# Layer 0's softmax weights in PSUM, and both node products of a pair in one bank: a four-layer graph network on one core

## The chip, the core and the metric

The kernel runs on one core of a Trainium2 chip. A core has a matrix engine (PE, with its weight loads shown apart as PEld), a vector engine (DVE), a scalar engine (ACT), a GpSimd engine (POOL) and a queue that only starts transfers (SP). They run side by side, each in its own program order, and wait for one another through semaphores. SBUF is the working memory with 128 partitions; PSUM is a small second memory, used here in banks of 512 float32 values per partition, into which PE writes its results, and which DVE and ACT read and write.

The metric is the device time of one execution in microseconds (us), as the median of several runs. Beside it there is one execution taken by the hardware profiler, with the start and duration of every instruction.

## The reference, cut to what matters

Four residual graph layers work on 6250 nodes and 100000 edges that are sorted by their target node. Layer 0 is a graph attention layer with eight heads. The change touches this layer and the work that prepares layer 1 from its result:

```python
h = jnp.maximum(_layernorm(x, axis=-1), 0.0)
x = x + _L0_gnn_ref(h, src, dst, ...)
# inside _L0_gnn_ref, after its own norm and x = x @ W_in + b_in:
scores_u = x @ W_u + b_u
scores_v = x @ W_v
e = scores_u[src] + scores_v[dst]
e = jnp.where(e >= 0, e, NEG_SLOPE * e)
m = jax.ops.segment_max(e, dst, num_segments=N_NODES)
ex = jnp.exp(e - m[dst])
s = jax.ops.segment_sum(ex, dst, num_segments=N_NODES)
probs = ex / s[dst]
xh = x.reshape(N_NODES, HEAD_DIM, N_HEADS)
msg = xh[src] * probs[:, None, :]
agg = jax.ops.segment_sum(msg, dst, num_segments=N_NODES)
return agg.reshape(N_NODES, DIM) @ W_ff + b_ff
# and then, for layer 1:
h = jnp.maximum(_layernorm(x, axis=-1), 0.0)
xw = h @ W
```

Layer 1 is a normalised sum over neighbours with a batch norm, layer 2 two single-head attention layers, layer 3 a pairwise interaction with a small network on the edges' attributes.

## The kernel before, in words

Nodes are ranked by their number of incoming edges and cut into 49 blocks of 128, one node per partition. `CAPS[b]` says how many neighbours a block holds per node: 44 for block 0, 25 for block 1, then falling to 9. For every block and neighbour slot one indirect transfer, issued by POOL, fetches 128 rows (one per partition) from a table in DRAM: `fetch` at L1623. It reads the 128 row numbers from a column of an index tile in SBUF (`k.ell` in layer 0). Layers 0, 1, 2a and 2b make 820 such fetches each, layer 3 another 882 of pair rows.

Layer 0 (L1627 to L1702) runs through `in_turns`, which interleaves three kinds of generators by hand. The order in which the generators emit instructions is the order on every engine; no scheduler rearranges them.

- `block0(b)`, one per block. First it issues the block's fetches into `rows` (three buffers; block 0 has a large one of its own). At the next block's first turn DVE forms the scores `e` of the fetched rows (L1656, L1657), their maximum (L1659) and the difference (L1660). One turn later ACT takes the exponential in place, `e` to `e`, both in SBUF (L1662). Another turn later DVE multiplies the rows by the weights (L1665, `rows` and `e`, result in `rows`), sums over the neighbours (L1669), sums the weights (L1670), and divides (L1671, L1673).
- `nodes0(b, a)`, one for each pair of blocks, appended to `tails` when the pair's sums are done. It multiplies the sums by `W_ff`, adds the result to the node rows `xp`, normalises, multiplies by layer 1's `W`, and writes layer 1's table `t1` (the profile's `l_t`). Each product is `times_in_hops`: transposes on PE into PSUM (L1092), three turns of waiting (`late`), a copy to SBUF on ACT (L1096), one turn, the matmul on PE (L1100), three turns. DVE reads the products from PSUM at L1640 and L1644.
- Background work through `behind`: `source_ranks`, which computes `k.ranks` for the next layers (its DVE lines L1372, L1374, L1375, L1386 and L1390 and PE line L1380), and from block 3 on `edge_weights`, the network on the edges for layer 3 (PE L1252 to L1274, ACT L1304 to L1315).

A block has `turns_of(b)` turns, four for most blocks, six for block 1. Layer 1's fetches read `t1`, so the first of them waits for the last pair's table rows.

PSUM in layer 0: `Banks(ps, 2, "g0_th")` holds two banks, taken in turn by successive products. A product's transposes lie in columns 0 to 255 of its bank, its matmul result in columns 256 to 511 of the same bank (`space=256`).

Layers 2a and 2b have the same block structure with one head. There ACT already writes the exponentials to a PSUM tile, and DVE's multiply (L1837) reads rows from SBUF and weights from PSUM:

```python
ex = weighed[:, b % 4, 0:n]
nc.scalar.activation(ex, e, AF.Exp, bias=s[:, 0:1])
e = ex
yield
v = rows[:, :n, 0:D]
nc.vector.tensor_tensor(v, v, e[:, :, None].to_broadcast([128, n, D]), op=ALU.mult)
```

Of the kernel before, what the change touches and what calls it, by code (L numbers as in the profile page):

```python
# [15 lines left out]
F32 = mybir.dt.float32  # L16
# [4 lines left out]
AF = mybir.ActivationFunctionType  # L21
# [6 lines left out]
N, D, E = 6250, 128, 100000  # L28
# [8 lines left out]
NH, HD = 8, 16  # L37
# [482 lines left out]
def load_cols(k, pool, a, name):  # L520
    t = pool.tile([D, a.shape[1]], F32, name=name)
    k.nc.sync.dma_start(t, a)
    return t
# [515 lines left out]
def norm_in_hops(k, p, x, got, name="nm"):  # L1039

    nc = k.nc
    nb = x.shape[1]
    mv = p.tile([128, nb, 2], F32, name=name + "_mv", bufs=3)
    for b in range(nb):
        st = p.tile([128, 6], F32, name=name + "_st")
        nc.vector.bn_stats(st, x[:, b, :])
        nc.vector.bn_aggr(mv[:, b, :], st)
    yield
    r = p.tile([128, nb, 2], F32, name=name + "_r", bufs=3)
    nc.scalar.activation(r[:, :, 0], mv[:, :, 1], AF.Sqrt, bias=k.eps)  # L1050
    yield
    nc.vector.reciprocal(r[:, :, 0], r[:, :, 0])
    nc.vector.scalar_tensor_tensor(r[:, :, 1], mv[:, :, 0], -1.0, r[:, :, 0], op0=ALU.mult, op1=ALU.mult)
    yield
    out = p.tile([128, nb, D], F32, name=name + "_h", bufs=3)
    got.append(out)
    for b in range(nb):
        nc.scalar.activation(out[:, b, :], x[:, b, :], AF.Relu, bias=r[:, b, 1:2], scale=r[:, b, 0:1])
    yield
# [22 lines left out]
        return self.tile[:, self.at]  # L1082


def times_in_hops(k, p, banks, h, w, width, got, late=1, space=512):

    nc = k.nc
    nb = h.shape[1]
    both = banks.next()
    t = both[:, 0:nb * 128].rearrange("p (b d) -> p b d", d=128)  # L1090
    for b in range(nb):
        nc.tensor.transpose(t[:, b, :], h[:, b, :], k.ident)  # L1092
    for _ in range(late):
        yield
    hT = p.tile([128, nb, 128], F32, name="th_T", bufs=3)
    nc.scalar.copy(hT, t[:, :nb, :])  # L1096
    yield
    y = both[:, space:512] if space < 512 else banks.next()
    for b in range(nb):
        nc.tensor.matmul(y[:, b * width:(b + 1) * width], lhsT=hT[:, b, :], rhs=w, start=True, stop=True)  # L1100
    got.append(y[:, 0:nb * width].rearrange("p (b f) -> p b f", f=width))
    for _ in range(late):
        yield


def with_scores(k, c, ps, w, scores, name):

    nc = k.nc
    n = sum(a.shape[1] for a in scores)
    full = c.tile([D, D + n], F32, name=name)  # L1110
    nc.sync.dma_start(full[:, 0:D], w)
    a = c.tile([D, n], F32, name=name + "_a")
    at = 0
    for s in scores:
        nc.sync.dma_start(a[:, at:at + s.shape[1]], s)
        at += s.shape[1]
    ty = ps.tile([128, 512], F32, name="tm_ty")
    nc.tensor.transpose(ty[:, 0:128], full[:, 0:D], k.ident)
    wT = c.tile([D, D], F32, name=name + "_t")
    nc.vector.tensor_copy(wT, ty[:, 0:128])  # L1120
    y = ty[:, 128:128 + n]
    nc.tensor.matmul(y, lhsT=wT, rhs=a, start=True, stop=True)
    nc.vector.tensor_copy(full[:, D:D + n], y)
    return full, a
# [375 lines left out]
def step(line):  # L1500

    return next(line, DONE) is not DONE


def finish(line):
    while step(line):
        pass
# [48 lines left out]
def by_rank(k, table, rows, b, nb=1):  # L1556

    k.nc.sync.dma_start(table[b * 128:(b + nb) * 128, :].rearrange("(b l) f -> l b f", l=128), rows)


def fast_layers(k, x, src, edges, l0, l1, l2a, l2b, l3):


    nc, tc = k.nc, k.tc
    gamma, beta, w_in, b_in, w_u, b_u, w_v, w_ff, b_ff = l0
    with ExitStack() as ctx:
# [11 lines left out]
        wf = load_cols(k, c, w_ff, "wf")  # L1578
        bf = load_row(k, c, b_ff, "bf", 128)
        w1 = load_cols(k, c, l1[0], "w1")  # L1580
        b1, g1, e1 = (load_row(k, c, a, n, 128) for a, n in zip(l1[1:], ("b1", "g1", "e1")))
        b2, b3 = load_row(k, c, l2a[3], "b2", 128), load_row(k, c, l2b[3], "b3", 128)
        with tc.tile_pool(name="fw_ps", bufs=1, space=PSUM) as ps:
            w2, _ = with_scores(k, c, ps, l2a[0], [a.rearrange("(p o) -> p o", o=1) for a in l2a[1:3]], "w2")
            w3, _ = with_scores(k, c, ps, l2b[0], [a.rearrange("(p o) -> p o", o=1) for a in l2b[1:3]], "w3")
# [40 lines left out]

        with tc.tile_pool(name="g0s", bufs=1) as q, tc.tile_pool(name="g0s_ps", bufs=1, space=PSUM) as qs, \  # L1627
                tc.tile_pool(name="g0", bufs=2) as p, tc.tile_pool(name="g0_ps", bufs=1, space=PSUM) as ps:
            banks = Banks(ps, 2, "g0_th")
            bigs = big.enter_context(tc.tile_pool(name="g0b", bufs=1, side="right"))  # L1630

            tails, sums = [], {}

            def nodes0(b, a):
                nb = a.shape[1]
                y, h = [], []
                xb = xp[:, b:b + nb, 0:D]
                nc.vector.tensor_tensor(xb, xb, bf[:, None, :].to_broadcast([128, nb, D]), op=ALU.add)
                yield from times_in_hops(k, p, banks, a, wf, D, y, 3, 256)
                nc.vector.tensor_tensor(xb, xb, y[0], op=ALU.add)  # L1640
                yield from norm_in_hops(k, p, xb, h)
                yield from times_in_hops(k, p, banks, h[0], w1, D, y, 3, 256)
                o = own[:, b:b + nb, 0:D]
                nc.vector.tensor_tensor(o, y[1], dinv[:, b:b + nb, None].to_broadcast([128, nb, D]), op=ALU.mult)  # L1644
                by_rank(k, t1[0:NP, :], o, b, nb)

            def block0(b):
                n = CAPS[b]
                nc.gpsimd.indirect_dma_start(
                    out=xp[:, b, :], out_offset=None, in_=xv,  # L1650
                    in_offset=bass.IndirectOffsetOnAxis(ap=k.node_i[:, b:b + 1], axis=0))
                rows = rows_tile(p, b, WE, D + NH, "g0_x", bigs)
                fetch(rows, t0, k.ell, b)
                yield
                e = (bigs if b == 0 else p).tile([128, n if b == 0 else WE, NH], F32, name="g0_e" + "b" * (b == 0))[:, :n, :]
                nc.vector.tensor_tensor(e, rows[:, :n, D:D + NH], xp[:, b, None, D:D + NH].to_broadcast([128, n, NH]), op=ALU.add)  # L1656
                nc.vector.scalar_tensor_tensor(e, e, SLOPE, e, op0=ALU.mult, op1=ALU.max)  # L1657
                s = p.tile([128, 3, NH], F32, name="g0_s")
                nc.vector.tensor_reduce(s[:, 0, :], e.rearrange("p w h -> p h w"), axis=AX.X, op=ALU.max)  # L1659
                nc.vector.tensor_tensor(e, e, s[:, 0:1, :].to_broadcast([128, n, NH]), op=ALU.subtract)  # L1660
                yield
                nc.scalar.activation(e, e, AF.Exp)  # L1662
                yield
                v = rows[:, :n, 0:D].rearrange("p w (d h) -> p w d h", h=NH)
                nc.vector.tensor_tensor(v, v, e[:, :, None, :].to_broadcast([128, n, HD, NH]), op=ALU.mult)  # L1665
                if b % 2 == 0:
                    sums[b // 2] = p.tile([128, min(2, NR - b), D], F32, name="g0_a")
                a = sums[b // 2][:, b % 2, :]
                nc.vector.tensor_reduce(a, rows[:, :n, 0:D].rearrange("p w d -> p d w"), axis=AX.X, op=ALU.add)  # L1669
                nc.vector.tensor_reduce(s[:, 1, :], e.rearrange("p w h -> p h w"), axis=AX.X, op=ALU.add)  # L1670
                nc.vector.reciprocal(s[:, 2, :], s[:, 1, :])  # L1671
                ah = a.rearrange("p (d h) -> p d h", h=NH)
                nc.vector.tensor_tensor(ah, ah, s[:, 2:3, :].to_broadcast([128, HD, NH]), op=ALU.mult)  # L1673
                if b % 2 or b == NR - 1:
                    tails.append(nodes0(b // 2 * 2, sums[b // 2]))

            ranks = source_ranks(k, q, qs)
            step(ranks)
            names = Pace(ranks, 0.22)

            def behind(b):
                if b == 3 and not hasattr(back, "weights"):
                    big.close()
                    begin_weights()
                    back.pace = Pace(back.weights, 0.07, 3, NR - 1)
                names(b)
                if hasattr(back, "pace"):
                    back.pace(b)

            in_turns([block0(b) for b in range(NR)], turns_of, behind, tails)  # L1690
            finish(ranks)
        named.close()
# [3 lines left out]
        with tc.tile_pool(name="g1s", bufs=1) as q, tc.tile_pool(name="g1s_ps", bufs=1, space=PSUM) as qs, \  # L1696
                tc.tile_pool(name="g1", bufs=2) as p:
            both = qs.tile([128, 512], F32, name="g1_both")
# [59 lines left out]
            with tc.tile_pool(name="g1_ps", bufs=1, space=PSUM) as ps:  # L1758
                banks = Banks(ps, 3, "g1_th")
# [30 lines left out]
        for name, table, bias in (("g2", t2, b2), ("g3", t3, b3)):  # L1790
            with tc.tile_pool(name=name, bufs=2) as p, tc.tile_pool(name=name + "_big", bufs=1) as bigs, \
                    tc.tile_pool(name=name + "_ps", bufs=1, space=PSUM) as ps:
                banks = Banks(ps, 3, name + "_th")


                weighed = ps.tile([128, 4, 128], F32, name=name + "_w")
# [245 lines left out]
```

## Time and profile before

| what | value |
|---|---|
| median of 3 runs | 8062.21 us (8047.26 to 8094.31) |
| the profiled execution's own time | 6335.19 us |
| its span, first to last instruction | 6333.0 us |
| POOL busy in the span | 4280.4 us, 68% |
| DVE busy | 3821.8 us, 60% |
| PE busy | 2837.1 us, 45% |
| ACT busy | 1182.8 us, 19% |

The stages, read from the first and last start of each table's fetches:

| stage | from to (us) |
|---|---|
| ranking of nodes, first node products | 0 to 455 |
| layer 0, block 0's fetches | 455 to 514 |
| layer 0, the other fetches | 514 to 1632 |
| layer 0's last pairs, no fetch under way | 1632 to 1656 |
| layer 1 | 1656 to 2684 |
| layer 2a, 2b, 3 | 2780 to 6333 |

How to read the views: a group of instructions has its source line, engine, operation, the tiles `out<-in` and the count, then the total busy time in us and the mean of one in ns, then the idle time of the engine just before them and what ended it. "Issue" is idle time in which the engine waited for nothing that the profile shows. In a timeline a row begins with start and duration in us. In a table of stretches each engine has its busy time and number of instructions.

The profiled execution is 1727 us shorter than the median of the runs; the trace does not show where that difference lies.

### The profile page before, as it was taken

To read this page: it belongs to the slowest core of one execution; us is meant where nothing else is said; L and a number is where in the kernel's file an instruction comes from. 1 tells how busy PE (TensorE), PEld (TensorE's weight loads), DVE (VectorE), ACT (ScalarE), POOL (GpSimd) and SP (SyncE) were. 2 spreads that over 40 slices of the span, in tenths; PEclk is the share of its full clock that TensorE was granted. 3 is DMA by queue.
4 is the path that set the end of the run, shared out by engine and by line. 5 is a ranking of instruction groups with operands and counts; after the bars stand their busy time and mean duration, and the time that the engine had idled before them with its cause. 6 is when DMAs were issued, how large, how long until landed. Compare 5 with 4: busy or idle time off the path is not lost. (4 is left out here: it accounts for less than half of the span.)

```text
span 6333.0 us, 46143 instructions
## 1 busy us (share of the span) xinstructions
PE 2837.1 (45%) x14116; PEld 1979.1 (31%) x14116; DVE 3821.8 (60%) x7136; ACT 1182.8 (19%) x2136; POOL 4280.4 (68%) x4403
## 2 busy tenths in 40 slices
PE   2320244444464774046555453234444346556555
PEld 2210132333243552034434111011111135555555
DVE  9744555665346942244333896688888646666666
ACT  0110122333221221023333010122222201001010
POOL 0037777777677777737777776667766567777775
PEclk9655566666677877557766676566666577887877
DMA  0124333333332332233333223899999943333333
GB/s 6 52 54 77 84 94 91 98 94 85 68 91 80 95 101 76 50 54 88 90 90 83 56 57 46 173 201 196 199 186 185 181 102 100 100 100 99 99 99 75
DMA packets 444362, 626.13 MB, mean 99 GB/s; under 512 B 81071, under 2 KB 334802, under 8 KB 434259
## 3 DMA queue, kind: packets, MB, share of 16 engines
q0 software_dynamic: 159296, 397.56, 26.9%
q1 hardware_dynamic: 284433, 224.86, 16.3%
q8 instruction: 115, 1.88, 0.1%
q14 instruction: 154, 1.26, 0.1%
q10 hardware_dynamic: 364, 0.57, 0.0%
HBM read 441.86 MB, written 180.80 MB: 98 GB/s over the span
## 5 line engine op out<-in xcount | busy, mean ns | idle before, releaser
L1894 POOL DMA_INDIRECT fp_rows<-pair_rows,ids x882 | 873.0, 990 | 289.5 <-issue 254.7
L1623 POOL DMA_INDIRECT g_x<-l_t,ell x776 | 822.4, 1060 | 236.5 <-issue 233.8
L1623 POOL DMA_INDIRECT g_x<-l_t,ranks x820 | 777.7, 948 | 274.0 <-issue 245.5
L1623 POOL DMA_INDIRECT g_x<-l2b_t,ranks x776 | 738.3, 951 | 295.1 <-issue 212.7
L1488 PE MATMUL sr_acc<-sr_t,sr_l 128*128 128x441 f16 x1640 | 558.6, 498 | 844.8 <-DVE sr_l L1481 761.4
L1623 POOL DMA_INDIRECT g_x<-l2a_t,ranks x776 | 735.7, 948 | 236.4 <-issue 231.8
L1912 PE MATMUL fp_qe<-own,fp_ot 128*128 128x128 f32 x1764 | 338.1, 363 | 494.7 <-DVE fp_pr L1919 494.5
L1273 PEld LDWEIGHTS ew_ps<-ew_r,ew_g 128*125 128x125 f32 x1600 | 389.9, 284 | 537.3 <-issue 523.0
L1488 PEld LDWEIGHTS <-sr_l 128*128 128x128 f16 x1640 | 172.8, 120 | 1218.7 <-DVE sr_l L1481 1044.1
L1712 DVE TENSOR_REDUCE g_s<-g_x 128x128 f32<-128x2432 f32 (+16 forms) x50 | 185.0, 3700 | 468.9 <-DMA g_x<-l_t,ranks 468.9
L1912 PEld LDWEIGHTS fp_qe<-own,fp_ot 128*128 128x128 f32 x1764 | 301.4, 263 | 522.4 <-DVE fp_pr L1919 517.6
L1273 PE MATMUL ew_ps<-ew_r,ew_g 128*125 128x128 f32 x1600 | 441.5, 372 | 0.0
L1274 PE MATMUL ew_ps<-ew_s,ew_g 128*125 128x128 f32 x1600 | 437.1, 369 | 0.0
L1899 DVE TENSOR_TENSOR fp_oh<-iota_l,fp_rows 128x768 f32<-128x768 f32 x147 | 141.0, 959 | 458.9 <-DMA fp_rows<-pair_rows,ids 458.9
L1842 DVE TENSOR_REDUCE g_a<-g_x 128x128 f32<-128x2048 f32 (+13 forms) x96 | 389.2, 4054 | 3.3
L1480 DVE TENSOR_SCALAR sr_t<-sr_it,sp_tile 128x882 f16<-128x882 f16 x820 | 385.5, 470 | 0.0
L1274 PEld LDWEIGHTS ew_ps<-ew_s,ew_g 128*125 128x125 f32 x1600 | 370.3, 284 | 0.0
L1270 PE MATMUL ew_ps<-ew_bias,ew_three 65*125 65x512 bf16 x200 | 103.9, 519 | 524.8 <-ACT ew_out L1315 524.8
L1908 ACT COPY fp_ot<-fp_tr 128x768 f32<-128x768 f32 x147 | 117.4, 799 | 1117.2 <-PE fp_tr L1904 1113.7
L1481 DVE TENSOR_SCALAR sr_l<-sr_it,sp_lane,sr_w 128x128 f16<-128x128 f16 x820 | 302.9, 369 | 8.2 <-POOL sr_w L1456 8.2
L1304 ACT ACTIVATE ew_g<-ew_ps,ew_c 128x500 f32<-128x500 f32 x200 | 135.4, 677 | 832.6 <-PE ew_ps L1265 831.7
L1380 PE MATMUL rk_ps<-rank_b,rk_oh 128*128 128x49 bf16 x1640 | 76.1, 211 | 443.7 <-DVE rk_pr L1372 437.8
(318 smaller groups left out, 6400.9 us busy)
## 6 DMA issues: line engine op xcount, KB each, us to landing
edge_rows<-ew_out SPq DMA_DIRECT2D x50, 910.0 KB
rk_row<-src_lanes SPq DMA_DIRECT2D x82, 320.0 KB
fp_rows<-pair_rows,ids POOLq DMA_INDIRECT x882
g_x<-l_t,ranks POOLq DMA_INDIRECT x820
g_x<-l_t,ell POOLq DMA_INDIRECT x776
g_x<-l2a_t,ranks POOLq DMA_INDIRECT x776
g_x<-l2b_t,ranks POOLq DMA_INDIRECT x776
ew_a<-in_edge_attr_dram SPq DMA_DIRECT2D x25, 448.0 KB
```

The source lines that it names most:

```text
L1273: nc.tensor.matmul(y[:EP, u * D:(u + 1) * D], lhsT=g[:, 0, e], rhs=m.r2, start=False, stop=False)
L1274: nc.tensor.matmul(y[:EP, u * D:(u + 1) * D], lhsT=g[:, 1, e], rhs=m.s2, start=False, stop=(u == 3))
L1304: nc.scalar.activation(g[:, i, :], h[:, i, 0:4 * EP], AF.Silu, bias=b)
L1480: nc.vector.tensor_scalar(t[:, i, :], it, k.tile3[:, cc:cc + 1], None, op0=ALU.is_equal)
L1481: nc.vector.tensor_scalar(l[:, i, :], it[:, 0:128], k.lane3[:, cc:cc + 1], weight[:, cc % KG:cc % KG + 1], op0=ALU.is_equal, op1=ALU.mult)
L1488: nc.tensor.matmul(acc[:, h, 0:HT], lhsT=l[:, i, :], rhs=t[:, i, h * HT:(h + 1) * HT], start=(cc % KG == 0), stop=end)
L1623: nc.gpsimd.indirect_dma_start(out=rows[:, j, :], out_offset=None, in_=table, in_offset=bass.IndirectOffsetOnAxis(ap=ids[:, at:at + 1], ax ...
L1712: nc.vector.tensor_reduce(s, rows[:, :n, :].rearrange("p w d -> p d w"), axis=AX.X, op=ALU.add)
L1842: nc.vector.tensor_reduce(a, v.rearrange("p w d -> p d w"), axis=AX.X, op=ALU.add)
L1894: nc.gpsimd.indirect_dma_start(out=rows[:, t, :], out_offset=None, in_=k.pairs, in_offset=bass.IndirectOffsetOnAxis(ap=k.ids[:, at:at + 1] ...
L1899: nc.vector.tensor_tensor(oh, k.iota_l[:, None, :].to_broadcast([128, TG, 128]), rows[:, :, D + 1:D + 2].to_broadcast([128, TG, 128]), op= ...
L1912: nc.tensor.matmul(qe[:, t, :], lhsT=ot[:, t, :], rhs=k.own[:, h, 0:D], start=True, stop=True)
```

## The change

The exponentials of layer 0 go to a PSUM tile `weighed` of one bank. Even blocks use columns 0 to 255, odd blocks columns 256 to 511. The DVE multiply and the sum of the weights then read the weights from PSUM; the scores `e` stay in SBUF up to the exponential. Block 0's 44 neighbours with 8 heads take 352 columns.

The number of banks stays at two: `nodes0` no longer has two of its own but one, `room`. The first product uses columns 0 to 255, the second columns 256 to 511, and a matmul's result is written over the transposes that it was made from. `times_in_hops` loses its `space` argument and gets `room`; with `room=None`, as in layers 1 and 2, it takes two banks in turn as it did. The last block stands alone (49 is odd), and its `nodes0` now lets four turns pass before it begins.

```diff
-def times_in_hops(k, p, banks, h, w, width, got, late=1, space=512):
+def times_in_hops(k, p, banks, h, w, width, got, late=1, room=None):
+
 
     nc = k.nc
     nb = h.shape[1]
-    both = banks.next()
-    t = both[:, 0:nb * 128].rearrange("p (b d) -> p b d", d=128)
+    t = banks.next() if room is None else room
+    t = t[:, 0:nb * 128].rearrange("p (b d) -> p b d", d=128)
     for b in range(nb):
         nc.tensor.transpose(t[:, b, :], h[:, b, :], k.ident)
     for _ in range(late):
         yield
     hT = p.tile([128, nb, 128], F32, name="th_T", bufs=3)
-    nc.scalar.copy(hT, t[:, :nb, :])
+    nc.scalar.copy(hT, t)
     yield
-    y = both[:, space:512] if space < 512 else banks.next()
+    y = banks.next() if room is None else room
     for b in range(nb):
         nc.tensor.matmul(y[:, b * width:(b + 1) * width], lhsT=hT[:, b, :], rhs=w, start=True, stop=True)
...
-            banks = Banks(ps, 2, "g0_th")
+
+            weighed = ps.tile([128, 512], F32, name="g0_w")
+            room = ps.tile([128, 512], F32, name="g0_th")
...
             def nodes0(b, a):
                 nb = a.shape[1]
+                if nb < 2:
+
+                    for _ in range(4):
+                        yield
                 y, h = [], []
                 xb = xp[:, b:b + nb, 0:D]
                 nc.vector.tensor_tensor(xb, xb, bf[:, None, :].to_broadcast([128, nb, D]), op=ALU.add)
-                yield from times_in_hops(k, p, banks, a, wf, D, y, 3, 256)
+                yield from times_in_hops(k, p, None, a, wf, D, y, 3, room[:, 0:256])
                 nc.vector.tensor_tensor(xb, xb, y[0], op=ALU.add)
                 yield from norm_in_hops(k, p, xb, h)
-                yield from times_in_hops(k, p, banks, h[0], w1, D, y, 3, 256)
+                yield from times_in_hops(k, p, None, h[0], w1, D, y, 3, room[:, 256:512])
...
-                nc.scalar.activation(e, e, AF.Exp)
+                ex = weighed[:, b % 2 * 256:b % 2 * 256 + n * NH].rearrange("p (w h) -> p w h", h=NH)
+                nc.scalar.activation(ex, e, AF.Exp)
+                e = ex
                 yield
                 v = rows[:, :n, 0:D].rearrange("p w (d h) -> p w d h", h=NH)
                 nc.vector.tensor_tensor(v, v, e[:, :, None, :].to_broadcast([128, n, HD, NH]), op=ALU.mult)
```

## The prediction

> **What bounds the kernel now.** The page's chain of waits explains nothing here (its shares round to 0%), so I began with the groups of instructions and looked for the engine that never rests.
>
> ```profile
> L1623 POOL DMA_INDIRECT g_x<-l_t,ell x776 | 822.4, 1060 | 236.5 <-issue 233.8 <-DMA g_x<-l_t,ell 2.4 <-DMA g_x_big<-l_t,ell 0.3
> L1623 POOL DMA_INDIRECT g_x<-l_t,ranks x820 | 777.7, 948 | 274.0 <-issue 245.5 <-DMA l_t<-own 24.0 <-DMA g_x<-l_t,ranks 4.5
> L1623 POOL DMA_INDIRECT g_x<-l2b_t,ranks x776 | 738.3, 951 | 295.1 <-issue 212.7 <-DMA g_x<-l2b_t,ranks 54.3 <-DVE sr_l L1481 16.4
> L1623 POOL DMA_INDIRECT g_x<-l2a_t,ranks x776 | 735.7, 948 | 236.4 <-issue 231.8 <-DVE sr_l L1481 0.9 <-DVE g_s L1844 0.9
> ```
>
> One source line, four layers. All of POOL's idle time before layer 0's fetches is "issue", 0.30 us between any two, and its 776 fetches with those gaps fill 822.4 + 236.5 = 1059 us of the stage's 1118 (the other 59 are the 48 fetches of `xp`). So POOL sets the pace of layer 0. And layer 0's fetch costs 1060 ns on average where the other layers pay 948 to 951. The timeline shows why; first layer 0, then layer 2a:
>
> ```profile
> 803.23 2.82 DVE L1665 TENSOR_TENSOR g_x<-g_x,g_e 128x2560 f32<-128x2560 f32 x1
> 804.33 2.53 POOL L1623 DMA_INDIRECT g_x<-l_t,ell  x1 [0.30 <-issue]
> 807.17 0.94 POOL L1623 DMA_INDIRECT g_x<-l_t,ell  x1 [0.31 <-issue]
> ...
> 2899.19 3.49 DVE L1837 TENSOR_TENSOR g_x<-g_x,g_w 128x3200 f32<-128x3200 f32 x1 [0.35 <-ACT g_w L1833]
> 2899.26 0.94 POOL L1623 DMA_INDIRECT g_x<-l2a_t,ranks  x1 [0.30 <-issue]
> 2900.50 0.94 POOL L1623 DMA_INDIRECT g_x<-l2a_t,ranks  x1 [0.30 <-issue]
> 2901.75 0.94 POOL L1623 DMA_INDIRECT g_x<-l2a_t,ranks  x1 [0.30 <-issue]
> ```
>
> Under L1665, both of whose inputs lie in SBUF, a fetch that starts is held until 0.8 us after the multiply has ended. Under L1837, the same multiply with its weights in PSUM, three fetches start and none is held. I counted this over the whole trace: 51 fetches start inside the 49 L1665s and last together 74.9 us more than 51 times 944 ns (the undisturbed fetch); 173 start inside the 98 L1837s, and their excess is -0.1 us. Of the 90 us that layer 0's fetches last too long, another 14.0 go to the rank work (L1372 6.2, L1390 5.3, L1386 2.5), which the change leaves alone.
>
> Next I asked whether anything else could take over. DVE's waits in 514 to 1632:
>
> ```profile
> DVE g_e L1656 <- DMA g_x<-l_t,ell: 285.8, 33, 13.3
> DVE g_e L1656 <- DMA xp<-xv_t,node_i: 120.5, 12, 15.0
> DVE g_e L1656 <- issue: 11.1, 2, 5.9
> DVE g_x L1665 <- ACT g_e L1662: 13.8, 23, 1.7
> ```
>
> Columns: total, times, longest. DVE spends 431 us of the stage waiting, all but 13.8 for fetches: 9.0 us in each of 48 blocks. It is the follower. The same stretch by engine, and the stage's end:
>
> ```profile
> 514.00:1632.00 1118.00, 397.56 (x2797) 295.31 (x2796) 654.32 (x1035) 272.68 (x424) 867.00 (x824) 0.60 0.36 90
> ...
> 1653.23 0.29 DVE L1644 TENSOR_TENSOR own<-g_th,dinv 128x128 f32<-128x128 f32 x1 [1.18 <-PE g_th L1100]
> ...
> 1655.86 0.94 POOL L1623 DMA_INDIRECT g_x<-l_t,ranks  x1 [24.02 <-DMA l_t<-own]
> ```
>
> PE is busy 36%, ACT 24%, DVE 59%, the DMA engines 36%. Only at the end does POOL wait for the others, 24 us, until the last node product has come through and its rows are written.
>
> **What the Trainium skill says.** "SBUF — State Buffer", section "Who interferes with whom": a DVE instruction with two SBUF inputs takes its second one through the read port that it shares with GpSimd, and holds up a GpSimd instruction that reads SBUF until it has finished. The trace agrees in both directions (74.9 us under 49 multiplies, none under 98). "PSUM — Partial Sum Buffer", section "PSUM bank collisions raise a hardware error": two engines must be kept apart by bank, not by address. So sharing a bank means more semaphore waits, and I looked for these. "VectorE: DVE Perf Modes", sections on the perf-mode tiers and the errata: a float32 multiply of two tensors has one speed wherever its inputs lie; a PSUM source costs 120 cycles of fixed time instead of 58, 65 ns at 0.96 GHz. The trace shows not even those 65 ns on the multiply, at equal shape:
>
> ```profile
> L1837 DVE TENSOR_TENSOR g_x<-g_x,g_w 128x2048 f32<-128x2048 f32 x10 | 22.7, 2271 | 0.3 <-ACT g_w L1833 0.3
> L1665 DVE TENSOR_TENSOR g_x<-g_x,g_e 128x2048 f32<-128x2048 f32 x5 | 11.4, 2288 | 0.5 <-ACT g_e L1662 0.5
> ```
>
> **The change part by part.**
>
> 1. The weights leave SBUF (L1662, L1665). Removes 74.9 us from POOL, which has no slack in this stage: -74.9. What is late next: nothing for 9.0 us per block; after the change a block takes 1.5 us less, so DVE keeps 7.5 us. DMA traffic rises from 90 to some 97 GB/s, and layers 2b and later run at up to 188. Fetches will now stand otherwise against the rank work; that term is 14.0 us today, and a third of it either way, 4.7, goes into the range.
>
> 2. L1670 reads PSUM with a step of 8 values. No row shows that form. Below, nothing; above, 65 ns by the price named, 49 times: 3.2 us of DVE, covered by its 9.0 us per block. If the cover were gone, +3.2. L1665 is the same: 0 to 3.2. I take 0.
>
> 3. ACT writes PSUM. The exponentials are 263 to 370 ns; a destination nearer or farther changes tens of ns, 49 times, behind DVE waits: 0. In the built program the semaphore wait sits on the table load ahead of the exponential for 42 blocks instead of 34, so for 8 blocks a 1.28 us load no longer runs ahead of the scores: 10.3 us of later exponentials altogether, again inside 9.0 us per block: 0; cover gone, +10.3.
>
> 4. `weighed` is one bank for two blocks. A new exponential must not meet DVE's reading of the last. But it already waits for its own L1660, which stands behind the last block's L1670 in DVE's order. No new wait: 0.
>
> 5. One bank for the node products. Before, two banks in turn; pairs overlap, one's first product with the other's second. In the program's order on PE, ACT and DVE nothing moves except around the last block, and node instructions wait for essentially the same instructions: already before, L1640 waits for the other pair's L1100 that stands just ahead of it. A gain from a freed wait is excluded, since nothing is freed. I take 0. The upper end is the rival below: behind a waiting L1640 on DVE stand the next block's scores, and behind these its row buffer, which POOL needs three blocks later.
>
> 6. Four turns for block 48. This lies in the 24 us at the end, where every wait counts. Its first product now stands behind the second of pair 46, on all three engines. Working with the rows of that stretch: pair 46's add ends at 1644.9, its normalised transposes at 1648.6; then block 48's copy 0.27, matmul 0.8, pair 46's matmul 1.22 (1650.9); then block 48's add, norm, transpose, copy, matmul, about 4.0. Its L1644 starts near 1655 instead of 1653.23: +2 (0 to 5). SP's one table write moves with it.
>
> Sum: -74.9 + 2 = -72.9 us against the profiled execution, 6335.19 (a span of 6333.0 and 2.2 around it) to 6262.3. Later stages start earlier as a whole: their order is fixed, layer 1 is POOL's again (1027 of its 1028 us busy or issuing), so nothing waits there for an old date. The median is 8062.21, 1727 us more, and the trace does not say where. If these microseconds lie outside layer 0, the same 72.9 come off: 7989.3. If they stretch everything by 1.27, the gain lies between 66.6 - 2 (a fetch every 1.59 us meets the multiply 0.17 us later, 49 times) and 1.27 x 74.9 - 2 = 93.1. I take 7989; with the spread of the three runs, about 20 us, this case's own range is 7945 to 8020.
>
> **The rivals.**
>
> - Half the gain, 8026. In the longer executions behind the median POOL waits for landings or buffers in layer 0, and part of the stalls lies under these waits. For: 1727 unexplained us. Against: in the trace POOL waits for nothing in that stage.
> - No gain, 8064. The stall isn't from the second input in SBUF but from something else about layer 0's multiply (its 32-byte pattern, its rate of writing), so it stays, plus item 6. Against: L1837 writes the same shapes in the same time and stalls nothing.
> - Slower, 8127. One bank chains the products of two pairs: DVE waits for PE at L1640 and L1644, and PE is in the middle of the edge network. The longest wait of ACT for a node product today is 11.9 us (copy behind L1092); if DVE had to wait so long twice per pair, 23.8, it would use up its 18 per pair and the 3.1 that the change saves, and lose 2.7 in each of 24 pairs, 65 us. It decides from 21.1 us per pair. Against: DVE waits for PE at these two lines only some 1 us in that stage today, under nearly the same waits.
>
> **How the numbers follow.** Chances: full gain 0.72, half 0.12, none 0.08, slower 0.08. About 0.5%, 40 us, is what a measurement can tell from no change. Full gain gives faster (0.70, with 0.02 within 0.5%), half gain is split (0.06 and 0.06), none is within. Together: faster 0.76, same 0.16, slower 0.08. The range takes the first two cases, 7945 to 8045, and leaves the last two out.
>
> **What would show it right or wrong.** Right: layer 0's fetches at about 963 ns, which is (822.4 - 74.9) / 776 (the 14 us of rank work remain), none over 2 us under L1674, the multiply of the new file; layer 0's fetches end near 1557 and layer 1's first starts some 26 us later; everything after is shifted by about 73 us and otherwise alike. Step 5 is wrong if DVE's waits for PE at the node products grow beyond a few us, or POOL shows waits other than "issue" in layer 0. Step 6 is wrong if the gap before layer 1 is far from 26. The prediction fails if the fetches still last 2.5 us under the multiply, or if the span falls by 73 and the median doesn't.

## The result, and the profile after

| kernel | median of 6 runs | lowest to highest |
|---|---|---|
| before | 8078.49 us | 8047.26 to 8094.31 |
| after | 8172.28 us | 8144.0 to 8203.73 |

The ratio is 1.0119, with a 95% interval of 1.0084 to 1.0153: slower by 94 us, where 73 us less were forecast. Every job (a set of runs taken together on one chip) ran at one of two levels, with the kernel before at 6290 to 6370 us or at 8060 to 8180 us, and these timed runs are of the high level, while the profile that the prediction was read from, 6335.19 us, is of the low one.

The page of the changed kernel has two lines that answer to the first ones shown before, and the last one is the same fetch in layer 1:

```profile
span 8170.3 us, 46134 instructions
...
L1624 POOL DMA_INDIRECT g_x<-l_t,ell x776 | 746.2, 962 | 656.8 <-DVE g_s L1679 426.5
L1624 POOL DMA_INDIRECT g_x<-l_t,ranks x820 | 812.7, 991 | 458.9 <-issue 249.8
```

The fetch of layer 0 lasts 962 ns on average, as forecast (963): the hold under the multiply is gone. Yet POOL now idles 656.8 us before these fetches, 426.5 of them for DVE, which has not yet released a row buffer. In the profile that the prediction used, POOL waited for DVE nowhere in this stage. What DVE waits for in that stretch, 516 to 1978 us of the kernel after (total, times, longest):

```profile
DVE rk_pr L1373 <- remote: 435.1, 20, 45.6
DVE xp L1647 <- PE g_th L1101: 148.0, 15, 35.6
DVE rk_pr L1373 <- issue: 134.5, 5, 51.0
DVE xp L1647 <- remote: 66.2, 4, 20.5
```

The four rows and three smaller ones (one of them 26.7 us) are 812 us, and all are at lines that read a product of PE. "Remote" means that a semaphore was raised at that moment and that no instruction ends there. One such wait in the timeline of all engines:

```profile
1220.83 0.67 PE L1381 MATMUL rk_ps<-rank_b,rk_oh 128*128 128x49 bf16 x20
...
1223.92 0.66 DVE L1391 TENSOR_TENSOR rk_ob<-iota_l,rk_hi 128x490 f32<-128x490 f32 x1
...
1228.41 1.22 PE L1101 MATMUL g_th<-wf,th_T 128*128 128x128 f32 x4 [6.92 <-issue]
...
1252.57 0.94 POOL L1656 DMA_INDIRECT xp<-xv_t,node_i  x1 [0.30 <-issue]
1258.84 0.67 DVE L1373 TENSOR_TENSOR rk_pr<-rk_ps,rk_ob 128x490 f32<-128x490 f32 x1 [34.26 <-remote]
1258.90 0.37 ACT L1097 COPY th_T<-g_th 128x256 f32<-128x256 f32 x1 [26.95 <-remote]
...
1277.17 0.94 POOL L1624 DMA_INDIRECT g_x<-l_t,ell  x1 [23.65 <-DVE g_s L1679]
```

Read it from the bottom. POOL waits 23.65 us for a buffer. DVE could not release it, because it stood for 34.26 us at L1373, which multiplies a result of the rank matmuls. PE's last group of these began at 1220.83 and PE did only four node matmuls after it, so what L1373 needs was finished, by the records, over 35 us before L1373 ran. ACT, which waits for other results of PE, was let go 0.06 us after DVE. Both came 5.3 us after POOL's last fetch had ended. In layer 0 of this profile, 35 waits of DVE for PE are over 5 us; 20 of them end between 3.4 and 7.4 us after POOL's last fetch, when POOL has run out of buffers. Another 11 end during one of POOL's fetches or within 1.4 us of its end.

The ends of matmuls come from a model, but the trace also records when PE raised its semaphore. For the rank group above, whose end is put at 1221.5, the raise stands at 1258.82, 0.02 us before L1373 starts. In this stage, 61 of 221 of PE's raises aren't on record within 5 us of the modelled end; in e6 below, a run of the same kernel at the low level, it is 1 of 224. A tenth of PE's raises are missing from this trace (1130 of 1252 are there), too few to make up the 61.

So two questions stand: does the kernel before show the same waits when it runs at 8100 us, and which part of the change makes them cost more?

### The profile page after: what moved, and what is told of

It is laid out like the page before. It is cut to its first block, busy times and chain, and to the rows that moved or that the text cites. A ratio compares the mean times of both kernels' runs of the same rounds, so it can differ in the third digit from the quotient of the medians.

```text
span 8170.3 us, 46134 instructions
## 1 busy us (share of the span) xinstructions
PE 2969.3 (36%) x14116; PEld 2033.6 (25%) x14116; DVE 3796.8 (46%) x7136; ACT 1179.9 (14%) x2136; POOL 4239.5 (52%) x4403
## 5 line engine op out<-in xcount | busy, mean ns | idle before, releaser
L1624 POOL DMA_INDIRECT g_x<-l_t,ell x776 | 746.2, 962 | 656.8 <-DVE g_s L1679 426.5
L1624 POOL DMA_INDIRECT g_x<-l_t,ranks x820 | 812.7, 991 | 458.9 <-issue 249.8
L1274 PEld LDWEIGHTS ew_ps<-ew_r,ew_g 128*125 128x125 f32 x1600 | 409.0, 297 | 1823.5 <-issue 1808.0
L1928 DVE TENSOR_TENSOR fp_pr<-fp_rows,fp_qe 128x256 f32<-128x256 f32 x441 | 183.4, 416 | 702.1 <-remote 666.1
L1846 DVE TENSOR_TENSOR g_x<-g_x,g_w 128x2048 f32<-128x2048 f32 (+13 forms) x96 | 233.9, 2437 | 585.7 <-ACT g_w L1842 491.6
L1274 PE MATMUL ew_ps<-ew_r,ew_g 128*125 128x128 f32 x1600 | 461.9, 386 | 12.5 <-issue 12.5
L1275 PE MATMUL ew_ps<-ew_s,ew_g 128*125 128x128 f32 x1600 | 458.2, 383 | 21.4 <-issue 21.4
L1941 PE MATMUL fp_acc<-fp_ms,fp_oh 128*128 128x128 f32 x1764 | 327.2, 317 | 228.4 <-issue 223.9
L1275 PEld LDWEIGHTS ew_ps<-ew_s,ew_g 128*125 128x125 f32 x1600 | 390.4, 298 | 21.9 <-issue 21.9
L1941 PEld LDWEIGHTS fp_acc<-fp_ms,fp_oh 128*128 128x128 f32 x1764 | 282.6, 229 | 252.3 <-issue 247.4
```

What stands on the lines that cost most here:

```text
L1274: nc.tensor.matmul(y[:EP, u * D:(u + 1) * D], lhsT=g[:, 0, e], rhs=m.r2, start=False, stop=False)
L1275: nc.tensor.matmul(y[:EP, u * D:(u + 1) * D], lhsT=g[:, 1, e], rhs=m.s2, start=False, stop=(u == 3))
L1624: nc.gpsimd.indirect_dma_start(out=rows[:, j, :], out_offset=None, in_=table, in_offset=bass.IndirectOffsetOnAxis(ap=ids[:, at:at + 1], ax ...
L1928: nc.vector.tensor_tensor(pr, rows[:, two, 0:D], qe[:, two, :], op=ALU.mult)
L1941: nc.tensor.matmul(acc, lhsT=oh[:, t, :], rhs=ms[:, t, :], start=(t0 + t == 0), stop=(t0 + t == TB - 1))
```

## The experiments

The expectations take the level for a property of the chip. It isn't: e14 and e15 ran at the low level on the chips that had shown the high one in e11 and e1, and e16 the other way round on the chip of e4 and e5. "Theory A" has one bank as the culprit, B the later stages, C the stream of POOL's fetches that holds PE's results back, D the weights in PSUM as such. In e3's expectation, B stands for node products that cost nothing.

**e1 and e2: both kernels unchanged, with profiles.**

> The kernel before, unchanged, with a profile that is to stand for its timed runs (the first profile, 6335 us, does not). Theory A (one bank lengthens the chain of DVE, PE and ACT in layer 0): time near 8078; layer 0's other fetches end about 94 us earlier than the 1958 us of the changed kernel, near 1864, and later stages last as long as in the changed kernel. Theory B (layer 0 gains its 75 us, the loss lies in later stages that the change doesn't touch): layer 0 ends near 2030 and the stages from layer 1 on are together about 170 us shorter than in the changed kernel. Both expect that this profile shows waits of 15 to 60 us of DVE for PE that the first profile lacks.

> The changed kernel once more, to see how far one profile's stage lengths repeat. Both theories: time 8144 to 8204, layer 0's other fetches end within some 20 us of 1958. If a stage's length moves by 90 us between two profiles of the same kernel, neither theory can be decided by stage lengths of single profiles.

Measured in one job, single executions: 8152.54 and 8274.05 us, 121.5 apart. Layer 0's other fetches end at 1895 and 2003, 108 apart. Every later stage agrees within 10 us. The loss lies in layer 0, and theory B is out. Both figures of e2 miss its expectation: 8274 us lies above the 8144 to 8204, and 2003 lies 45 us past 1958. That 1958 was the end of the last `xp` fetch; the last `g_x` fetch of the first profile after is at 1978. So a stage repeats to some 25 us (1487 us against 1462), well under the 90 that would have left the theories undecided.

The waits of DVE in the kernel before at the high level (516 to 1895):

```profile
DVE xp L1640 <- remote: 310.6, 12, 40.6
DVE rk_pr L1372 <- remote: 260.5, 22, 51.9
DVE xp L1640 <- PE g_th L1100: 92.4, 6, 31.5
DVE rk_pr L1372 <- issue: 52.2, 4, 23.3
```

and POOL's in the same stretch:

```profile
POOL g_x L1623 <- issue: 228.4, 749, 0.3
POOL g_x L1623 <- DVE g_a L1669: 191.1, 13, 31.0
POOL g_x L1623 <- DVE g_s L1670: 105.1, 9, 13.5
```

The reader is to compare with the prediction's view of the same kernel, where DVE waits for fetches and POOL for nothing. Here DVE waits 721 us for PE (its smaller waits included) and POOL 296 us for DVE. The roles are exchanged before anything is changed. The late results are there too: of 31 waits of DVE for PE over 5 us, 15 end between 3.1 and 6.3 us after POOL's last fetch.

**e3: the node products alone.** The diff against the kernel after:

```diff
-            weighed = ps.tile([128, 512], F32, name="g0_w")
...
-                ex = weighed[:, b % 2 * 256:b % 2 * 256 + n * NH].rearrange("p (w h) -> p w h", h=NH)
-                nc.scalar.activation(ex, e, AF.Exp)
-                e = ex
+                nc.scalar.activation(e, e, AF.Exp)
```

> The kernel before with only the node products changed: one bank, product over its transposes, four turns for block 48; the exponentials stay in SBUF. Theory A: this part carries the loss, and the stalls of the fetches remain, so the time is 8172 or above, up to 8250 (ratio to before 1.011 to 1.021). Theory B (this part costs nothing): within 20 us of 8078, ratio 0.998 to 1.003, and the exponentials in PSUM carry the loss.

Measured (high level): ratio to before 0.9993, interval 0.9972 to 1.0013. Layer 0's other fetches take 1394 us, against 1379 in e1 and 1487 in e2. One bank and the four turns cost nothing by themselves; theory A is out. What is left of the change is the exponentials in PSUM, alone or together with the one bank: no run has them in PSUM beside two banks. They take the hold off POOL. Whether the lost hold makes the layer longer, or the place of the weights, is what e4 and e5 ask.

**e4 and e5: the exponentials stay in PSUM, and POOL's stream is slowed on purpose.** e4, after each fetch (`idle` is a scratch tile in SBUF):

```diff
-                fetch(rows, t0, k.ell, b)
+                for j in range(n):
+                    fetch(rows[:, j:j + 1, :], t0, k.ell, b, j, 1)
+                    nc.gpsimd.memset(idle, 0.0)
```

e5, once per block, with a tile of 900 instead of 224 values:

```diff
-                fetch(rows, t0, k.ell, b)
+                m = n // 2
+                fetch(rows[:, 0:m, :], t0, k.ell, b, 0, m)
+                for _ in range(2):
+                    nc.gpsimd.memset(idle, 0.0)
+                fetch(rows[:, m:n, :], t0, k.ell, b, m, n - m)
```

> The changed kernel with a POOL memset of 128x224 bf16 (about 0.27 us) after every fetch of layer 0, so that fetches start at least 1.5 us apart instead of 1.25. Theory C (PE's finished products reach DVE and ACT late because POOL's stream of fetches runs ahead of what the transfers' path drains[...]; a slower stream lets them through): DVE's waits for PE in layer 0 fall from 818 to 1000 us... that is from 818 us to below 300, POOL's waits for DVE from 427 to 449 us to below 150, and the stage from 516 us to its last fetch takes about 1250 us (776 fetches at 1.5 us, 48 at 1.25, some waits) instead of 1462 to 1487; time below the kernel before, ratio about 0.975. Theory D (reads and writes of the weights in PSUM hold up PE's products; POOL has no part in it): the waits stay and 776 memsets with their gaps, 210 to 260 us, come on top wherever POOL isn't waiting; the stage takes 1500 us or more, ratio 1.01 to 1.03.

> The changed kernel with two POOL memsets of 128x900 bf16 in the middle of each block's fetches, together about 1.8 us: a pause about as long as the hold under the multiply of the kernel before, at a place of its own. Theory C: the pause does the work of the lost hold; layer 0 goes back to 1379 to 1410 us and the ratio to about 1.000. Theory D: the weights are still in PSUM, the stage stays at 1462 to 1487 us, ratio 1.010 to 1.014. If only the place of the hold counts (it comes with the multiply, 4 us ahead of the pair's transposes), the result is that of theory D too, and e4 tells the two apart.

Measured: 6363.69 us for e4 (before 6306.76; ratio 1.0093, interval 1.0076 to 1.0110) and 6305.82 us for e5 (0.9997, 0.9989 to 1.0006). The job ran at the low level, where neither theory had made a forecast, so nothing about C or D follows. It tells something else: at this level POOL sets the pace. The pause of e5 costs what the hold had cost, and the ratio is 1.

**e6 to e8: the kernel after, and both again.**

> The changed kernel. The chip decides what this run can tell. On a chip where the kernel before takes about 6307 us (as in e4 and e5): the prediction's sum, -73 us, ratio 0.988 to 0.990, POOL without waits for DVE in layer 0. On a chip where it takes 8060 to 8160 us: ratio 1.010 to 1.014 again. A rival (the change costs time on every chip, and the first profile was only luck): ratio above 1.005 on both.

> As e4, the changed kernel with a memset after every fetch of layer 0. On a chip near 6307 us: 1.009 again. On a chip of 8060 to 8160 us: theory C (a slower stream of fetches lets PE's products through) 0.975, layer 0's other fetches 516 to about 1766 us, DVE's waits for PE there under 300 us; theory D (the weights in PSUM are what delays) 1.01 to 1.03, the waits stay at 800.

> As e5, one pause of about 1.8 us per block in the changed kernel's fetches. On a chip near 6307 us: 1.000 again. On a chip of 8060 to 8160 us: theory C 0.998 to 1.003; theory D, or if the hold matters only where the multiply puts it, 1.010 to 1.014.

Measured, again at the low level: the kernel after 6209.84 us against 6292.08, ratio 0.9872 (0.9856 to 0.9889), a little more than the 0.988 to 0.990 expected; e7 1.0093 (1.0076 to 1.0110), e8 0.9999 (0.9990 to 1.0007). The change is 82 us faster here. The rival in e6's expectation, a loss at every level, is out. Of e6, the page and DVE's and POOL's waits in layer 0:

```profile
L1624 POOL DMA_INDIRECT g_x<-l_t,ell x776 | 744.7, 960 | 236.5 <-issue 230.4
```

```profile
DVE g_e L1663 <- DMA g_x<-l_t,ell: 214.8, 30, 10.8
DVE g_e L1663 <- DMA xp<-xv_t,node_i: 119.0, 14, 12.1
...
DVE xp L1647 <- PE g_th L1101: 1.6, 1, 1.6
```

```profile
POOL g_x L1624 <- issue: 230.4, 756, 0.3
POOL g_x L1624 <- DMA l_t<-own: 23.0, 1, 23.0
```

Same program as e2, nearly the same fetch (960 ns, 962 in e2), and almost none of the waits: DVE waits for fetches and some 4 us for node products, POOL only at the very end.

**e9 to e16: the same two kernels until the high level came.** e9 (1.0091) and e10, e12, e13, e14, e15 (0.9999 to 1.0001) fell on the low level and repeat e7 and e8. The other two answer the question.

> The same kernel as e9 with the same expectations: on a chip where the kernel before takes 8060 to 8160 us theory C expects 0.975 and waits of DVE for PE under 300 us in layer 0, theory D 1.01 to 1.03 and waits of 800; on a chip near 6300 us 1.009 again.

Measured at the high level: 8018.24 us against 8177.26, ratio 0.9818 (0.9775 to 0.9861). From 516 to the last fetch it takes 1262 us, shorter than the kernel before. POOL's groups in layer 0:

```profile
L1624 POOL DMA_INDIRECT g_x<-l_t,ell x776 | 747.8, 964 | 214.2 <-issue 133.2 <-DVE g_s L1682 80.4 <-DVE rk_pr L1373 0.3
L1663 POOL MEMSET g_idle<- 128x224 bf16 x781 | 242.7, 311 | 0.5
```

and DVE's largest waits for PE:

```profile
DVE xp L1648 <- remote: 172.1, 13, 31.9
DVE rk_pr L1373 <- remote: 157.6, 18, 28.1
```

A fetch now comes every 1.45 us instead of 1.25 ((747.8 + 242.7 + 133.2) / 776). POOL has 243 us more to do and the layer is 200 to 225 us shorter than in the kernel after, because POOL's waits for DVE fall from 427 to 80. DVE's waits for PE are 452 us, 56% of 812, but not below the 300 that theory C named; the direction holds, its size was too hopeful, and so was the ratio of 0.975. Theory D expected the opposite sign, and the weights are still in PSUM.

> The same kernel as e10, hoped for on a chip where the kernel before takes 8060 to 8180 us. Theory C as it now stands (POOL's stream holds PE's signals back, e11): a pause of 1.8 us per block, like the lost hold, brings layer 0's other fetches from 516 back to 1379 to 1410 us and the ratio to 0.998 to 1.003. If e11 helped only through the spacing of the single fetches, and not through the sum of pauses, or if the weights in PSUM have a cost of their own: 1.008 to 1.014. On a chip near 6300 us: 1.000 again.

> The same kernel as e12 with the same expectations. On a chip where the kernel before takes 8060 to 8180 us: 0.998 to 1.003 and layer 0's other fetches in 1379 to 1410 us if the sum of POOL's pauses counts, 1.008 to 1.014 and 1462 to 1487 us if it doesn't or if the weights in PSUM have a cost of their own. On a chip near 6300 us: 1.000 again.

> As e15: on a chip of 8060 to 8180 us 0.998 to 1.003 and 1379 to 1410 us if the sum of POOL's pauses counts, otherwise 1.008 to 1.014 and 1462 to 1487 us; on a chip near 6300 us 1.000 again.

e16 fell on the high level: 8043.56 us against 8064.25, ratio 0.9978 (0.9956 to 1.0000), 1344 us from 516 to the last fetch, a little less than theory C's 1379 to 1410.

```profile
L1624 POOL DMA_INDIRECT g_x<-l_t,ell x776 | 746.8, 962 | 449.3 <-DVE g_s L1684 224.3 <-issue 222.0 <-DMA g_x<-l_t,ell 1.2
L1664 POOL MEMSET g_idle<- 128x900 bf16 x96 | 82.5, 859 | 2.8
```

85 us of pauses take 202 us of POOL's waits for DVE away (427 to 224), and the loss is gone with the weights still in PSUM. But the pauses are longer than what they stand for. At the high level POOL often waits while DVE multiplies: in e1 only 27 fetches start inside the 49 multiplies, and they are held for 47 us together, not for 74.9. An estimate by length, from the 118 to 143 us that 85 us of pauses take off the stage, gives 65 to 79 us for a pause of 47, where the change cost 83 to 108. The rest, 4 to 43 us, is about what two profiles of one kernel differ by (25 us), so the weights need no cost of their own, but a small one isn't excluded. A run with the same pauses and the weights in SBUF, at the high level, would decide it; there is none. Nor is it shown how a pause helps: of the 29 waits of DVE for PE over 5 us in e16, only 4 end during a pause.

The profiles of the high level together, layer 0 from 516 us to its last fetch. DVE's waits are all its idle time just before a line that reads a product of PE. I split each wait of POOL for a buffer where the last wait of DVE for PE (of over 2 us) inside it ends; waits of POOL with none inside are left out (1 to 13 us in all):

| kernel | stage, us | fetch, ns | DVE waits for PE | POOL: last fetch to DVE let go | DVE let go to next fetch |
|---|---|---|---|---|---|
| before, e1 | 1379 | 1021 | 721 | 110 | 174 |
| one bank, e3 | 1394 | 1017 | 702 | 127 | 180 |
| after | 1462 | 962 | 812 | 201 | 225 |
| after, e2 | 1487 | 962 | 804 | 214 | 236 |
| even pace, e11 | 1262 | 964 | 452 | 24 | 53 |
| one pause, e16 | 1344 | 962 | 646 | 71 | 145 |

Both parts of POOL's wait grow with the change, the first by more: 110 to 201 and 214. This fits POOL, unhindered, using up its buffers earlier and then sitting until PE's results come through, but it doesn't prove it. If the waits are split at the first long wait of DVE instead of the last, the first part goes from 110 only to 134 and 142, and the second from 174 to 293 and 308.

## Why the prediction was wrong

**The step that failed** is the transfer of the sum to the median. The text gave two cases for the 1727 us between profile and median: "If these microseconds lie outside layer 0, the same 72.9 come off", or "if they stretch everything by 1.27", a gain between 64.6 and 93. Neither holds. Of the 1817 us between e1 and that profile, 263 lie in layer 0 (1379 us against 1116), and they aren't a stretch of the work: an undisturbed fetch lasts 0.94 us in the timelines of both levels, DVE is busy 654 us of the stage in the first profile and 649 in e1, and PE, the only one to slow down, 398 and 415. The rest are waits, of DVE for PE and of POOL for DVE. Where POOL waits 296 us for DVE, 47 or 75 us less work on POOL need gain nothing. "POOL sets the pace of layer 0" and "DVE is the follower" were true of the execution that was profiled and false of the runs that were to be forecast. The 21% between the two stood in the text, and I let it widen a range rather than ask whether another engine might set the pace.

The remaining steps:

1. Weights out of SBUF. The mechanism is right at both levels (fetch 962 and 960 ns, 963 forecast), its value only at the low one. There layer 0's fetches end at 1553 (1557 forecast), and the kernel gains 82 us (72.9 forecast). At the high level the hold was smaller (47 us in e1) and worth less than nothing, since a stall of POOL there is also a pause. The slack that this item gave DVE, 9.0 us per block, was read a little high: it counts 24.9 us of idle time that didn't wait for fetches, and without them it is 8.5.
2. The sum of the weights from PSUM, taken as 0 with an upper end of +3.2 (65 ns more for each): it became faster, 92 ns less at equal shape, see the end. Hidden, as forecast.
3. The exponential's destination: 0, right. DVE's multiply waited 15.1 us for ACT in the first profile and 15.1 in e6.
4. `weighed` in one bank, no new wait: right. In e6 the waits ahead of the exponential still end with DVE's difference (L1667) or a node's norm, never with a read of the last block's weights.
5. One bank for the node products, 0: right, 0.9993 in e3. The stage's waits at L1647 and L1640 look like the slower rival's, and e3 shows that they don't come from the bank.
6. Four turns for block 48, +2: the gap before layer 1 is 23.0 us in e6, 24.0 before. So -1, where 26 were expected.

Of the rivals, "half the gain" came nearest in its reason, POOL waiting for buffers in the longer executions. But a wait that hides a gain was its worst case; that the stall might be useful was in none. The slower rival had the sign and nearly the size (8127) by a mechanism that e3 excludes.

Shown: the loss lies in layer 0, it needs the exponentials in PSUM, and it goes with a pause or a slower stream on POOL; PE's raises are recorded late at the high level. Argued only: that POOL's stream is what holds them back, that the lost hold is the whole cause, and by what path. No run looked at the path itself. Open is also what puts a job on one level or the other. One thing differs between the levels in every run: PE's granted clock, its mean share of full speed, is 0.675 to 0.689 at the low level and 0.625 to 0.637 at the high one. In layer 0 PE's busy time differs by 18 us and the stage by 263, so slower matmuls alone don't fill it; whether the clock is a cause or a result isn't known. No version beats both kernels at both levels: even pace gains 1.8% at the high one and loses 0.9% at the low one, where the kernel after gains 1.3%.

## What to carry to other kernels

If the profiled execution's own time is far from the median, the profile may have another pace-setter than the timed runs: take a second profile whose time agrees, or give the exchange of roles a large share of the chance. Here a stall on an engine that runs ahead had become a pause in which the others caught up, so ask what a faster stream will do when it reaches the end of its buffers. And a part of a change that looks risky (one bank in place of two) is tested alone before it is blamed.

## What was not expected of the hardware

At the high level PE's results reach DVE and ACT late: up to 51.9 us for DVE in layer 0 (e1), up to 68.3 us for ACT in layer 1 (the kernel after). The largest wait of all looks the same and isn't. It lies outside the change: after layer 1's 820 fetches DVE needs a sum from PE (L1754), with no fetch left to issue. First the kernel after, then DVE's wait in e6:

```profile
3256.29 0.43 DVE L1737 TENSOR_TENSOR g_sums<-g_sums,g_d 106x256 f32<-106x256 f32 x1
...
3681.17 0.71 PE L1754 MATMUL g_both<-g_sums,ones 128*128 128x128 f32 x4
3681.92 0.42 DVE L1757 TENSOR_SCALAR g_sums<-g_both 128x256 f32<-128x256 f32 x1 [425.20 <-PE g_both L1754]
```

```profile
DVE g_sums L1757 <- PE g_both L1754: 1.3, 1, 1.3
```

DVE starts 0.04 us after PE's matmul has ended, so nothing is late here: PE comes to the sum late. Ahead of it in PE's order stand 93 groups of the edge network. In e6 all 93 run during layer 1; in the kernel after only 40 do, and the other 53 fill the 425 us (PE is busy 292 of them). The wait is the backlog of a whole layer. In e1 it is 430.9 us.

The profiles of the high level also miss records: of DVE's 5633 instructions that raise its semaphore, 3917 raises are in the trace of the kernel after and 5628 in that of e6; of the records of landed transfers, 18208 and 78041. So at that level the views can be wrong about who ended a wait, and the readings above rest on the line at which an engine stands, and for how long. Whether the missing records and the late results have one cause isn't known.

DVE's sum of the weights, which reads with a step of 8 values, is faster from PSUM than from SBUF in this kernel. First the kernel before, then e6, by shape:

```profile
L1670 DVE TENSOR_REDUCE g_s<-g_e 128x8 f32<-128x128 f32 x5 | 1.9, 371 | 0.0
```

```profile
L1679 DVE TENSOR_REDUCE g_s<-g_w 128x8 f32<-128x128 f32 x5 | 1.4, 279 | 0.0
```

A quarter less at equal shape, 4.6 us over the layer's 49 blocks (17.8 + 0.8 against 14.0).
